# Moving the token choice of a sparse attention layer into the loop of the gated delta rule before it

## The chip, the cores and the metric

The kernel runs on one core of one Trainium2 chip, in one launch, on fp32 data. The time is device time in microseconds (us) of that core. A core has five engines, and each works through its own list of instructions in order: TensorE (PE: matrix products and transposes, with PEld for its weight loads), VectorE (DVE), ScalarE (ACT: functions such as exp and sigmoid), GpSimd (POOL, which here also issues the indirect DMAs) and SyncE (SP, which only issues DMAs). Data meet only through semaphores, so an instruction that is not ready holds back all that stand behind it on its engine.

## The reference

The program is four layers, each added to the residual stream `x` of 8 sequences x 512 tokens x 256 channels after a layer norm: a gated mixer with its MLP, a mixture of eight experts with two per token, a gated delta rule, and an attention over chosen tokens. The last two matter here, cut to what they compute (`B` is 8, `T` 512, `D` 256):

```python
# gated delta rule: 8 heads, keys of 128, values of 64
x_ = layernorm(x)
beta = 2 * sigmoid(x_ @ Wb)
alpha = exp(-exp(A_log) * softplus(x_ @ Wa + dt_bias))
q, k = l2norm(silu(conv4(x_ @ Wq))), l2norm(silu(conv4(x_ @ Wk)))
v = silu(conv4(x_ @ Wv))
for t in range(T):          # state: 64 x 128 per head
    state = alpha[t] * (state - beta[t] * outer(state @ k[t], k[t])) + beta[t] * outer(v[t], k[t])
    out[t] = state @ q[t]
x = x + (out * rsqrt(mean(out * out) + 1e-5) * o_norm_w * silu(x_ @ Wg)) @ Wo

# attention over chosen tokens: 16 heads of 16
z = layernorm(x)
gate = sigmoid(z @ mWg)                 # one number per token
idx = top_k(gate, 256)                  # half of the tokens of each sequence
c = z[idx]
o = softmax((c @ mWq) @ (c @ mWk).T / 4) @ (c @ mWv) @ mWo      # per head
y = zeros(T, D); y[idx] = o * gate[idx]
out = x + y
```

What the attention needs in order to choose its tokens (layer norm, gates, ranks) depends on the delta rule's output of that one sequence, and on nothing of the other sequences.

## The kernel before

The four layers follow one another in one program. Python functions lay down the instructions, and the framework's scheduler fixes each engine's final order, derives the semaphores, and maps tile pools to memory; a pool keeps `bufs` buffers per tag, and a new tile of a tag waits until the oldest one's readers are done. Line numbers are those of the profile of this kernel.

**The delta rule** (`delta_rule`, from L566) takes each sequence in two groups of 4 heads, so it has 16 groups, n = 0 to 15; even n is a sequence's first group, odd n its second. Tokens are cut into 4 tiles of 128. Per group: `channels` ("c" in the order below) projects and convolves (PE `pc` L681, ACT L683, three DVE taps per chunk L685); `norms` ("n") takes the lengths of the keys and queries, through tiles of the tag "sq"; `fade` ("e") makes the decay masks on POOL and PE (L728 and after); `prepare` ("p") makes the 128 x 128 lower triangles of key products, one DVE product per head and tile (`NQ`, L748); `inverses` ("i") inverts the triangles block by block: POOL and ACT copy the diagonal 32-blocks (`own`, L776), DVE turns them (`low`), solves blocks of 8 and 16 rows in a long chain of small operations, and turns the result (`dn`, L763), after which PE multiplies ever larger blocks (`pn` L831 first). `sides` ("v") transposes values and keys (`ptv`, `ptk`, then the DVE products `r` and `K`, L914); `advance` ("a") runs the recurrence over the 4 tiles (`pkq` L950, `pw` L957, `state`); `silus` ("g") makes the output gates; `outputs` ("o") squares (`oq`, a tile of a tag with one buffer), normalises (L988 to L996), projects and adds to the residual tile `cx` (L1009), and after the second group stores the sequence to HBM (`xbufs[1]`, L1012). `load` ("t" or "l") brings in a coming sequence: the residual tile, eight indirect gathers `yg` of the experts' results on POOL with their DVE adds, the layer norm `cz` and its transposes.

While group n advances, group n+1 is prepared and inverted and group n+2 projected. All of these are generators. A string of letters, written by hand, says in which order they are stepped within one group of the loop; what is left is drained at the group's end. The string sets the order in which instructions are laid down, from which the scheduler makes each engine's list.

**The attention** (`chosen_attention`, from L1100) is a pipeline over the sequences with six parts, each a generator, at lags of 0 to 5 steps: `norm` loads a sequence `dx` and centres it (`dz`), one step ahead of the others; `place` (lag 0) transposes `dz` (`ptd`, L122), multiplies it with the gate weights repeated over 128 columns (`gate_all`, PE `pgt` L1167), so that every partition holds the gates of all 512 tokens as a row, takes the sigmoid, extracts the gates as a column (POOL product with the identity `dg` L1171, DVE reduction), ranks each token by comparing its gate with all the others (`ahead`, and `rank` L1186, once per tile of 128 tokens), and scatters the rows of `dz` to their ranks in HBM (`placed`, four indirect DMAs on POOL, L1193); the first 256 rows are then loaded as `c` (L1195). `project` (lag 1) transposes `c` (`pct` L1207) and makes queries, keys and values; `maxima` (lag 2) takes the row maxima of the scores (`sc` L1250, DVE reductions L1252) and folds them into the queries; `sums` (lag 3) makes the transposed scores, exponentials (ACT) and weighted sums; `finish` (lag 4) divides, projects (`pdy` L1311), stores the result, and gathers each token's row of it (`got`, L1317 on POOL; a token that was not chosen gets a row of zeros); `leave` (lag 5) multiplies by the gate, adds to `dx` (L1324) and stores the output. A second string of letters orders the parts within a step. The loads and stores of `dx`, `c`, `result` and the output are on SP's queue, weights on ACT's.

Of the kernel before, what the change touches and what calls it, by code (L numbers as in the profile page):

```python
# [14 lines left out]
F32 = mybir.dt.float32  # L15
# [5 lines left out]
P = 128  # L21
# [24 lines left out]
def block(ctx: ExitStack, tc: tile.TileContext, a: dict, out: bass.AP):  # L46
# [518 lines left out]

    def delta_rule():  # L566
        with ExitStack() as cx:
# [21 lines left out]
            V.tensor_scalar(wo, wo, onw, None, ALU.mult)  # L589

# [422 lines left out]

            seqs = {}
# [35 lines left out]
            def drain(*work):  # L1050
# [9 lines left out]
                p v t p v p l a v p t l a v p a p a p l a p a p a i l a i g a i c l g i a a e i l a g i e c i a a i l e g e  # L1060
# [13 lines left out]
            for n in range(total):  # L1074
# [4 lines left out]
                if n % 2 == 0 and coming is not None:  # L1079
                    work["t"] = coming  # L1080
                elif n + 3 < total:
                    work["l"] = coming = load(n // 2 + 2)
                else:
                    coming = None
                for k in order:
# [9 lines left out]
                drain(*work.values())  # L1095

# [3 lines left out]
    def chosen_attention():  # L1100
# [4 lines left out]
        with ExitStack() as cx:  # L1105
            wp = cx.enter_context(tc.tile_pool(name="d_w", bufs=1))
            gate_w = wp.tile([P, DK, 1], F32, name="gate_w")
# [4 lines left out]
            for t, n in ((gate_w, "mWg"), (wq, "mWq"), (wk, "mWk"), (wv, "mWv"), (wo, "mWo")):  # L1112
                nc.scalar.dma_start(t, a[n].rearrange("(c p) f -> p c f", p=P))
            gate_all = wp.tile([P, DK, P], F32, name="gate_all")
            V.tensor_copy(gate_all, gate_w.to_broadcast([P, DK, P]))
# [16 lines left out]
            placed = [dram.tile([T, D], F32, name=f"placed{b}") for b in range(B)]  # L1132
# [16 lines left out]
            zs, rows, chosen, qkv, outs, gots = {}, {}, {}, {}, {}, {}  # L1149

            def norm(b):
                x = tk.tile([P, NT, D], F32, name=f"dx{b}", tag="x", bufs=8)
                nc.sync.dma_start(x, rows_of(xbufs[1][b]))
                z = tk.tile([P, NT, D], F32, name=f"dz{b}", tag="z", bufs=3)
                center(sm, x, z, f"d{b}")
                zs[b] = x, z
                yield

            def place(b):


                x, z = zs.pop(b)
                xT = tk.tile([P, DK, T], F32, name=f"dxT{b}", tag="xT")
                turn(pf, "pf", z, xT, f"d{b}")
                ps = pf.tile([P, T], F32, name=f"pgt{b}", tag="pf")
                for k in range(DK):
                    TE.matmul(ps, gate_all[:, k, :], xT[:, k, :], start=k == 0, stop=k == DK - 1)  # L1167
                row = tk.tile([P, NT, P], F32, name=f"row{b}", tag="row")
                S.activation(row, ps, AF.Sigmoid)
# [222 lines left out]
```

## Time and profile before

| what | value |
|---|---|
| median of 3 runs | 3389.84 us (3385.32 to 3393.04) |
| the profiled execution's own time | 3389.93 us |
| its span, from first to last instruction | 3388.2 us |
| mean granted TensorE clock | 0.912 |
| mixer, MLP and experts, 0 to 1520 us | PE busy 1419.7 us |
| delta rule, 1520 to 2918.4 us | PE busy 1224.5, DVE 919.3, ACT 869.2, POOL 316.6 us |
| attention, 2918.4 to 3388.2 us | PE busy 366.6, DVE 208.6, ACT 139.2, POOL 85.4 us |

The profile is of one execution; it lies 1.7 us in span below its own time, and its own time is at the median. An answer by stretches gives, for each, the length, then busy us and the number of instructions of PE, PEld, DVE, ACT and POOL, then the granted TensorE clock (1.00 is full), the busy share of the DMA engines, and GB/s. In a row of waits, the engine and line that wait stand first, then what ended the wait, then us in total, times, and the longest. In a timeline, a row has the start in us, the duration, the engine, the line, the operation with output and inputs, and in brackets the idle time before it with its releaser. In a row of groups, after the bar, stand busy us, mean ns of one, and idle time before. Busy DVE or POOL does not mean that these bound the kernel; what counts is which wait ends last in a stretch.

### The profile page before, as it was taken

The numbers are of one execution on the slowest core, as the hardware profiler recorded it, in microseconds if no ns is written. First come the engines' busy times: TensorE is split into PE (matmuls) and PEld (weight loads), VectorE is DVE, ScalarE is ACT, GpSimd is POOL, SyncE is SP. The second block draws the span as 40 slices with busy tenths as digits, with TensorE's granted clock in tenths as the row PEclk, the third lists the DMA queues.
The fourth block names the chain that finished last, engine by engine and source line by source line (L and its number), as shares of the span: only waits on it lengthen the run. The fifth ranks groups of instructions, "written<-read, shape, count | busy, mean of one in ns | idle before, by whom it ended". The sixth has DMA issues, their size and how long they took to land. (4 is left out here: it accounts for less than half of the span.)

```text
span 3388.2 us, 59510 instructions
## 1 busy us (share of the span) xinstructions
PE 3010.9 (89%) x24662; PEld 2224.0 (66%) x24662; DVE 1891.7 (56%) x4375; ACT 1545.9 (46%) x2747; POOL 632.1 (19%) x669
## 2 busy tenths in 40 slices
PE   7999999889999999995889898989889899498887
PEld 3655555445999999982567666666666667366664
DVE  4555545334555555555557777677776664554432
ACT  3554442112333333335457667667676764233322
POOL 1000003541010000013112313222221110212111
PEclk8999999999999999997779899989899897687787
DMA  5000003220588888881000000000000000201111
GB/s 205 13 25 13 13 13 145 69 70 19 225 324 332 334 328 314 332 322 41 2 1 20 8 20 8 20 8 25 3 23 2 8 2 8 92 24 40 37 40 47
DMA packets 97133, 302.69 MB, mean 89 GB/s; under 512 B 12760, under 2 KB 79456, under 8 KB 87648
## 3 DMA queue, kind: packets, MB, share of 16 engines
q0 software_dynamic: 19440, 221.19, 17.3%
q1 hardware_dynamic: 68016, 68.44, 6.0%
q10 hardware_dynamic: 9408, 9.27, 0.8%
q8 instruction: 194, 3.18, 0.4%
q14 instruction: 75, 0.61, 0.1%
HBM read 248.79 MB, written 50.08 MB: 88 GB/s over the span
## 5 line engine op out<-in xcount | busy, mean ns | idle before, releaser
L444 PE MATMUL p_r<-zT,w 128*128 128x128 f32 x4544 | 534.4, 276 | 7.1 <-DMA w<-in_experts,wrow 6.7
L444 PEld LDWEIGHTS p_r<-zT,w 128*128 128x128 f32 x4544 | 526.4, 192 | 12.5 <-issue 7.8
L685 DVE SCALAR_TENSOR_TENSOR cy<-pc,conv,cy 128x509 f32<-128x509 f32 (+2 forms) x480 | 351.4, 740 | 141.5 <-ACT cy L683 136.5
L448 ACT ACTIVATE t_r<-p_r,w 128x128 f32<-128x128 f32 x568 | 170.4, 373 | 266.5 <-PE p_r L444 181.6
L444 PE MATMUL p_s<-sxT,shared_w 128*128 128x512 f32 x512 | 222.8, 595 | 1.7 <-ACT sxT L124 1.7
L449 DVE SCALAR_TENSOR_TENSOR l_r<-p_r,w,t_r 128x128 f32<-128x128 f32 x284 | 79.9, 343 | 175.6 <-PE p_r L444 175.6
L444 PEld LDWEIGHTS p_s<-sxT,shared_w 128*128 128x128 f32 x512 | 96.9, 191 | 121.7 <-issue 108.1
L508 POOL DMA_INDIRECT w<-in_experts,wrow x71 | 67.0, 943 | 579.6 <-ACT sg_r L457 568.3
L681 PE MATMUL pc<-cxT,wq 128*128 128x512 f32 x256 | 153.1, 724 | 15.8 <-DVE cy L685 13.6
L681 PE MATMUL pc<-cxT,wk 128*128 128x512 f32 x256 | 143.5, 654 | 7.2 <-DVE cy L685 3.9
L304 PE MATMUL pp<-hT,win 128*128 128x512 f32 x320 | 144.3, 603 | 0.2 <-ACT hT L126 0.2
L522 PE MATMUL pyr<-w,htr 128*128 128x256 f32 x568 | 134.5, 380 | 2.6 <-DVE htr L462 2.6
L449 DVE SCALAR_TENSOR_TENSOR g_r<-p_r,w,t_r 128x128 f32<-128x128 f32 x284 | 80.0, 344 | 101.2 <-PE p_r L444 101.2
L683 ACT ACTIVATE cy<-pc,conv 128x512 f32<-128x512 f32 x160 | 108.3, 685 | 60.3 <-PE pc L681 58.9
L728 POOL TENSOR_TENSOR e<-le,g 128x512 f32<-128x512 f32 x64 | 66.5, 1046 | 363.6 <-DVE NQ L748 341.0
L746 PE MATMUL pk<-kq 128*128 128x256 f32 x512 | 130.4, 391 | 0.7 <-DVE NQ L748 0.4
L748 DVE SCALAR_TENSOR_TENSOR NQ<-pk,nbk,e 128x256 f32<-128x256 f32 x256 | 110.0, 477 | 27.4 <-PE pk L746 27.0
L394 PE MATMUL pf<-hT,fc 128*128 128x512 f32 x256 | 122.8, 607 | 0.0
L457 ACT ACTIVATE sg_r<-g_r 128x512 f32<-128x512 f32 x71 | 44.8, 631 | 159.8 <-DVE g_r L455 159.8
L399 PE MATMUL pj<-pj,sT 128*128 128x256 f32 x512 | 113.1, 379 | 0.0
L522 PEld LDWEIGHTS pyr<-w,htr 128*128 128x128 f32 x568 | 102.5, 190 | 13.7 <-issue 2.7
L950 PEld LDWEIGHTS pkq<-state,kq 128*128 128x128 f32 x768 | 95.6, 197 | 24.1 <-DVE state L972 16.7
(393 smaller groups left out, 6217.5 us busy)
## 6 DMA issues: line engine op xcount, KB each, us to landing
zt<-zbuf SPq DMA_DIRECT2D x71, 128.0 KB
ybuf<-yt SPq DMA_DIRECT2D x71, 128.0 KB, 3.2
zbuf<-zeros SPq DMA_DIRECT2D x11, 768.0 KB, 11.0
x<-in_x SPq DMA_DIRECT2D x8, 512.0 KB
xbuf<-x SPq DMA_DIRECT2D x8, 512.0 KB, 2.9
sx<-xbuf SPq DMA_DIRECT2D x8, 512.0 KB, 3.9
xbuf<-sx SPq DMA_DIRECT2D x8, 512.0 KB, 2.9
cx<-xbuf SPq DMA_DIRECT2D x8, 512.0 KB, 9.4
```

Of the source, the lines that this page charges most:

```text
L304: TE.matmul(ps, win[:, k, m : m + P], hT[:, k, :], start=k == 0, stop=k == DK - 1)
L394: TE.matmul(ps, fc[:, k, f * P : (f + 1) * P], hT2[:, k, :], start=k == 0, stop=k == DK - 1)
L399: TE.matmul(ps, sT[:, f, t * P : (t + 1) * P], pj[:, f, :], start=f == 0, stop=f == 7)
L444: last_of[0] = TE.matmul(ps[:, f, :], wx[:, k, (f0 + f) * P : (f0 + f + 1) * P], xin[:, k, :], start=k == 0, stop=k == DK - 1)
L448: S.activation(t3[:, f, :], p3[:, f, :], AF.Identity, bias=b3[:, f0 + f : f0 + f + 1])
L449: V.scalar_tensor_tensor(t1[:, f, :], p1[:, f, :], b1[:, f0 + f : f0 + f + 1], t3[:, f, :], ALU.add, ALU.mult)
L522: last_of[0] = TE.matmul(ps, hT[:, f, :], w2[:, f, :], start=f == 0, stop=f == 3)
L681: TE.matmul(ps, w[:, k, n * P : (n + 1) * P], xT[:, k, :], start=k == 0, stop=k == DK - 1)
L683: S.activation(y, ps, AF.Copy, scale=conv[:, at + n, 3:4])
L685: V.scalar_tensor_tensor(y[:, j:], ps[:, : T - j], conv[:, at + n, 3 - j : 4 - j], y[:, j:], ALU.mult, ALU.add)
L746: TE.matmul(pk[:, j, :, :], kq[:, h + j, 0, ts], kq[:, h + j, :, ts], start=True, stop=True)
L748: V.scalar_tensor_tensor(NQ[:, :, t * HG + h + j, :], pk[:, j, :, :], s.nbk[:, t, h + j : h + j + 1], bc(e[:, h + j, :], 1, 2), ALU.mult, ...
```

## The change

The token choice of a sequence leaves the attention and is done in the delta rule's loop. The new `place` gets the residual tile `cx` of a sequence whose second group is done, still in memory, and works for it during the next sequence's first group: for n = 2, 4, ..., 14 it places sequence n/2 - 1. The last sequence is placed after the loop. Its steps are the letter "w", which is put into the order at seven places, all of them early (only even groups have such work).

How the gates are made changes too: instead of a transposition and PE products, DVE multiplies `dz` by the gate weights, loaded repeated over the partitions, and sums over the channels, which gives the gates as a column; ACT takes the sigmoid in place; PE turns the column, repeated to 128 columns, into the row by four transposes, and ACT copies it. Ranking and scattering are as before. The tiles share buffers with the delta rule's: `dz` the tag of `oq` and `cz`, the products and the row the tag "sq", `ahead` that of the inverses' "tmp", the transposes the banks of `ptv`, `ptk` and the others.

Gates and clipped ranks are kept for all sequences in tiles that last (`seat_gate`, `seat`), and `placed` is allocated ahead of both layers. In the attention, `norm` and `place` are replaced by `fetch`, which issues the loads of `c` and `dx` one step ahead; `gate_all` and its matmuls go, the lags shrink by one, and the loop has B + 4 steps. `dx` has 7 buffers, not 8.

```diff
+    seat_gate = [cst([P, NT], f"sgate{b}") for b in range(B)]
+    seat = [const.tile([P, NT], mybir.dt.int32, name=f"seat{b}") for b in range(B)]
+    placed = [dram.tile([T, D], F32, name=f"placed{b}") for b in range(B)]
...
+            gate_w = wp.tile([P, D], F32, name="gate_w")
+            nc.scalar.dma_start(gate_w, a["mWg"].rearrange("d o -> (d o)").partition_broadcast(P))
...
+            def place(b, x):
+                z = tk.tile([P, NT, D], F32, name=f"dz{b}", tag="oq")
+                center(sm, x, z, f"d{b}")
+                yield
+                prod = ch.tile([P, NT, D], F32, name=f"dg{b}", tag="sq", bufs=2)
+                V.tensor_mul(prod, z, bc(gate_w, 1, NT))
+                col = seat_gate[b]
+                V.tensor_reduce(col, prod, AX.X, ALU.add)
+                S.activation(col, col, AF.Sigmoid)
+                pt = pt_.tile([P, NT, P], F32, name=f"prow{b}", tag="pt")
+                for t in range(NT):
+                    TE.transpose(pt[:, t, :], col[:, t : t + 1].to_broadcast([P, P]), ident)
+                row = ch.tile([P, NT, P], F32, name=f"row{b}", tag="sq", bufs=2)
+                S.copy(row, pt)
+                yield
+                rank = sm.tile([P, NT], F32, name=f"rank{b}", tag="rank")
+                for t in range(NT):
...
+                    V.tensor_reduce(rank[:, t : t + 1], ahead.rearrange("p t s -> p (t s)"), AX.X, ALU.add)
+                    yield
...
+                V.tensor_copy(seat[b], rank)
+                for t in range(NT):
+                    G.indirect_dma_start(placed[b], bass.IndirectOffsetOnAxis(ap=at[:, t : t + 1], axis=0), z[:, t, :], None)
+                yield
...
-                p v t p v p l a v p t l a v p a p a p l a p a p a i l a i g a i c l g i a a e i l a g i e c i a a i l e g e
+                p w v t w p v w p w l a v w p t l a w v p w a p a p l a p a p a i l a i g a i c l g i a a e i l a g i e c i a a i l e g e
...
+                if n % 2 == 0 and n > 0:
+                    work["w"] = place(n // 2 - 1, done)
...
+                done = s.x
+            drain(place(B - 1, done))
...
-            gate_all = wp.tile([P, DK, P], F32, name="gate_all")
-            V.tensor_copy(gate_all, gate_w.to_broadcast([P, DK, P]))
...
+            def fetch(b):
+                c = chosen[b] = tk.tile([P, NS, D], F32, name=f"c{b}", tag="c")
+                nc.sync.dma_start(c, placed[b][0:C1, :].rearrange("(s p) d -> p s d", p=P))
+                x = tk.tile([P, NT, D], F32, name=f"dx{b}", tag="x", bufs=7)
                 nc.sync.dma_start(x, rows_of(xbufs[1][b]))
...
+                rows[b] = x, seat_gate[b], seat[b]
...
-            parts = {"p": (place, 0), "s": (sums, 3), "m": (maxima, 2), "q": (project, 1), "f": (finish, 4), "l": (leave, 5)}
...
-            for n in range(B + 5):
+            parts = {"s": (sums, 2), "m": (maxima, 1), "q": (project, 0), "f": (finish, 3), "l": (leave, 4)}
+            fetch(0)
+            for n in range(B + 4):
+                if n + 1 < B:
+                    fetch(n + 1)
...
-                for k in "p s q l m f p s q f m f s f p s q m q p s q m p m s q p m n f".split():
+                for k in "s q l m f s q m f m s f s q m q s q m m s q m f".split():
```

The old `norm` and `place` of the attention, and the `z`, `xT`, `dg` and `ahead` tiles that they used there, are taken out; the work of `project`, `maxima`, `sums`, `finish` and `leave` stays as it was.

## The prediction

> **What bounds the kernel now.** I read the page's busy shares first, then the stages by time, then the waits of the two stages that the change touches, then their timelines.
>
> ```profile
> PE 3010.9 (89%) x24662; PEld 2224.0 (66%) x24662; DVE 1891.7 (56%) x4375; ACT 1545.9 (46%) x2747; POOL 632.1 (19%) x669
> ...
> 2323.00:2368.00 45.00, 44.90 (x281) 35.33 (x280) 34.01 (x89) 27.31 (x39) 18.34 (x19) 1.00 0.13 42
> 2368.00:2376.50 8.50, 0.31 (x10) 0.17 (x13) 8.43 (x16) 5.51 (x8) 6.30 (x5) 0.69 0.10 31
> 2376.50:2390.00 13.50, 11.65 (x398) 8.52 (x400) 7.97 (x18) 10.77 (x17) 0.00 (x0) 0.56 0.02 4
> ...
> PE pn L831 <- DVE dn L763: 47.1, 7, 8.4
> ...
> 2357.35 2.17 POOL L776 COPY own<-NQ 32x512 f32<-32x512 f32 x2 [1.34 <-DVE NQ L748]
> ...
> 2375.64 0.70 DVE L763 STREAM_TRANSPOSE dn<-cols 128x512 f32<-128x512 f32 x1
> ...
> 2917.96 0.42 DVE L1009 TENSOR_TENSOR cx<-py,cx 128x256 f32<-128x256 f32 x1 [1.44 <-PE py L1008]
> ...
> 2952.87 0.98 POOL L1193 DMA_INDIRECT placed<-dz,at  x1 [1.71 <-DMA placed<-dz,at]
> ...
> 2955.54 0.96 POOL L1193 DMA_INDIRECT placed<-dz,at  x1 [1.70 <-DMA placed<-dz,at]
> ...
> 2963.50 1.09 PE L1207 MATMUL pct<-ident,c 128*128 128x128 f32 x4 [20.40 <-DMA c<-placed]
> ...
> 2925.00:2960.00 35.00, 8.26 (x24) 4.16 (x24) 30.48 (x117) 10.23 (x16) 8.10 (x8) 0.60 0.48 152
> ...
> L1186 DVE TENSOR_REDUCE rank<-ahead 128x1 f32<-128x512 f32 x32 | 21.7, 677 | 0.2
> ...
> L1167 PE MATMUL pgt<-dxT,gate_all 128*128 128x512 f32 x32 | 17.2, 657 | 1.0 <-ACT dxT L124 1.0
> ...
> L122 PE MATMUL ptd<-ident,dz 128*128 128x128 f32 x64 | 10.2, 298 | 15.9 <-DVE dz L115 15.6 <-ACT row L1169 0.2
> ```
>
> PE is the busiest engine, but the stages differ. The delta rule runs from about 1524 to 2918 us in 161 us per sequence (the stores of a finished sequence start at 2162.6, 2323.5, 2484.1). The three stretches are the start of one sequence's first group, the place that receives the new work. For 45 us PE is full (44.9) at clock 1.00, while DVE is busy 34.0: DVE has 11.0 us free. Then PE stands still for 8.2 us. The wait names the cause: the first small matmul of the blockwise inverse (L831) waits for the DVE transpose `dn`, and DVE is full (8.43 of 8.50). The chain is: last NQ product on DVE, its diagonal copied by POOL and ACT (`own`, 2357.35), a long DVE chain, `dn` at 2375.64. All first groups but one show the gap: 8.2, 8.4, 8.2, 8.2, 8.2, 4.6 and 1.4 us from the second sequence to the eighth; their sum is the 47.1 us of the wait. So in this very stretch DVE, not PE, sets the end.
>
> The chosen attention runs from the last add at 2918.4 to 3388.2. The first 45.1 us of it, to the first `pct` transpose at 2963.50, are the normalising, ranking and scattering of the first sequences with PE at 8.26 us of 35. After that PE works 83 to 88% of each 50 us.
>
> [...] after the 8.2 us gap the clock is 0.56 for 13.5 us. [...] the page's loads show 1283 ns. [...] a scatter of 0.97 us is followed by the next only 2.67 us after its start, since it waits for the landing.
>
> **The change part by part.** *Out of the attention's startup.* The last sequence's placing is not overlapped: it is drained after the loop, and in the built order the load of `c0` waits for that sequence's fourth scatter to land, though its own data are long there, because its buffer lies where the closed pools were; all of SP's later loads and PE's `pct` are behind it. So the startup shrinks and does not vanish. From 2918.4: last statistics 0.57, root 0.30, reciprocal 0.17, four `dz` 1.36, product 1.22, reduction 1.21 (the 1024-wide one at L992), table load and sigmoid 1.50, four transposes 0.8, row copy 0.59, ranking 6.2 (7.6 by the rows below, less the overlap of neighbours), cast 0.18, four scatters one landing after another 10.7 (4 x 2.67), load 2.8. Sum 27.6, against 45.1: gain 17.5.
>
> *Out of the attention's steps.* PE loses the turning (10.2) and the gate matmuls (17.2), 27.4 in all, of which 8.26 are in the startup: 19.1 remain. Two table loads a sequence (9.0 + 6.4 us on ACT) go, which hold back the exponentials that free the score banks; I take 1 us for each of six sequences, 6. DVE's ranking goes too, but DVE was mostly off the path. A stall stays: each full step stops PE at the second half's scores (7.3, 5.6, 4.4, 6.1, 2.0, 4.4 us), because DVE holds the add of the gathered result ahead of the maxima. In the new order this add stands at the head of the next step, again about 10 us after its output; I take no change, bounds +15 and -15. Fewer pipeline stages: the step that goes is the startup, already counted. Gain 42.5, bounds 28 to 58. The `dx` and `c` loads move on SP's queue; their 5 us land far ahead of use.
>
> *Into the delta rule, seven times.* DVE per sequence, by the attention's rows over 8: statistics and `dz` (12.2 + 4.7 + 1.3 + 11.9)/8 = 3.8; product 1.2; reduction 1.2; ranking (21.7 + 11.6 + 10.9, and 16.7 for the comparisons of 128 to 384 columns)/8 = 7.6; casts 0.5. Together 14.3, and 12.3 of occupancy, as 34 neighbours overlap by some 0.06 (four `dz` take 1.36, not 1.62). PE gets four transposes, 0.45; ACT 2.4 with one more table load, under PE's work. The scatters' bytes fall where DMA is 5% busy.
>
> DVE is in order, and the built order puts all of it between the previous sequence's last add and NQ's second half. There 11.0 us are free, but in pieces that wait for PE. I walk the new order with these durations, in us from that add (2322.97), in brackets where the trace of before has the same instruction end:
> - `dz` done 6.9, product 8.5, reduction 10.0, sigmoid after its table load 12.7.
> - PE reaches the four transposes at 14.4. They wait for the sigmoid; `ptv`, `ptk` and `pab` are queued behind them. Row copied 15.6; ranks done 19.5, 22.4, 25.8, 28.7, each with the step's own DVE work between.
> - `r` 22.8 (17.6), so `pw` waits 2.0 on PE; `state` 29.2 (22.2), `pkq` waits 1.0; `g` 30.8 (26.9); last NQ 37.8 (34.3), 3.6 late.
> - POOL: scatters at 29.6, 33.4 (two fade products between), 36.1, 38.8, each waiting for the landing before it. Behind them stand the third fade product, `own` and the gathers. `own` ends 42.3 (36.6), 5.7 late; DVE's `low` waits for it.
> - From `low` to `dn` the built order also has the output's reduction and a convolution tap (1.2 + 0.7), which stood behind `dn` before: 7.6 late. The next sequence's gathers start at 46.9 and land 3 later; their adds stand in the inverse's chain, where DVE comes at 47.0 and, with a part made good later, loses 2.1: 9.7, say 9.5.
>
> What is late next is `pn`, PE's next work, and with it the rest of the sequence, in which PE is nearly full: nothing there gives it back. Five sequences at 9.5 are 47.5; the seventh place has no gathers of a next sequence beside it, the eighth no convolutions either: 7.5 and 5. Loss 60. From below: all 11.0 free us are used, the excess is 1.3, with the 1.9 moved ahead 3 each, 21. From above: nothing is hidden, 12.3 + 1.9 = 14 each, 98.
>
> The gate weights' broadcast load lies among a dozen loads on ACT's queue at the stage's start: 0.5.
>
> Sum: 3389.9 (the profiled execution, span 3388.2 and 1.7 around it; the median is 3389.8) + 60 - 42.5 = 3407.
>
> **The rivals.** *DVE swallows it, faster:* the ranking fills DVE's holes and the loss is about 3 each, 21, with a gain of 47: 3364. For it: DVE is 72% busy over the sequence (115.6 of 161). Against: only the 45 us before the gap count. It decides from a loss under 6 us per sequence (42.5 over 7). *POOL becomes the bound, slower:* the scatters, each behind the landing of the one before, hold `own`, the fades and the gathers, 14 each, 98, gain 42: 3446. For it: 10.7 us of POOL per sequence where a group has few holes. Against: before, POOL is busy 18 of these 45 us. *The two cancel:* about 6 each, 3390; DVE's holes take half.
>
> **How the numbers follow.** Forecast 3407, own range 3397 to 3432, chance 0.45; POOL bound 0.15; swallowed 0.27; cancel 0.13. Under 0.2% (7 us) a measurement of this kernel can't tell a change. Faster 0.27, same 0.13, slower 0.60. For 8 in 10 I leave out the outer parts of the first two rivals: 3361 to 3441.
>
> **What would show it.** The gap before `pn` in first groups grows from 8 to 11 or more, and the distance of stores from 161 to about 170; `own` starts just after the fourth scatter; the first `pct` comes 28 us after the last add, not 45; from there to the end about 400 us instead of 425. I am wrong if the gap stays near 8 (then faster), if `c0` doesn't wait for the scatters, or if the stall at the scores goes or doubles.

## The result, and the profile after

The changed kernel takes 3419.22 us (median of 4 runs, 3411.78 to 3426.13), the kernel before 3391.23 (median of 4). The ratio is 1.0083, 95% interval 1.0068 to 1.0099: slower by 0.8%. The profiled execution is the fastest of the four, 3411.78 us with a span of 3409.8, so its sums stand 7.4 us below the median.

By stages, in the two profiled executions:

| stage | before | after | difference |
|---|---|---|---|
| to the last add of the delta rule | 2918.4 | 3000.0 | +81.6 |
| from there to the first `pct` | 45.1 | 29.8 | -15.3 |
| from there to the end | 424.7 | 380.0 | -44.7 |
| span | 3388.2 | 3409.8 | +21.6 |

The page of the changed kernel, then busy time by stretches: three of the first group of the fifth sequence (the one shown of before; it now begins at 2361.6), and the attention from its first `pct`.

```profile
PE 3011.3 (88%) x24598; PEld 2206.6 (65%) x24598; DVE 1907.1 (56%) x4382; ACT 1531.9 (45%) x2732; POOL 630.2 (18%) x661
...
2361.60:2401.20 39.60, 37.86 (x238) 30.16 (x235) 33.49 (x90) 21.57 (x35) 9.80 (x11) 1.00 0.11 37
2401.20:2413.00 11.80, 8.68 (x43) 5.30 (x42) 7.26 (x19) 7.96 (x11) 9.41 (x10) 1.00 0.11 33
2413.00:2425.10 12.10, 0.09 (x5) 0.04 (x6) 12.10 (x21) 4.48 (x7) 7.52 (x7) 0.60 0.15 43
3029.80:3409.80 380.00, 331.57 (x2272) 222.61 (x2272) 124.10 (x208) 107.79 (x201) 40.09 (x48) 0.84 0.15 44
```

Before, PE was full for 45 us and then stood still for 8.2. Now it has 46.5 us of work in 51.4 and then stands still for 12.1, with DVE at 12.10 of 12.10. The waits give the sum over all groups, 66.1 us in place of 47.1, with the same seven waits; the timeline shows the cause in this group.

```profile
PE pn L840 <- DVE dn L772: 66.1, 7, 13.0
...
2361.14 0.42 DVE L1018 TENSOR_TENSOR cx<-py,cx 128x256 f32<-128x256 f32 x1
...
2390.79 1.06 POOL L1058 DMA_INDIRECT placed<-dz,at  x1 [0.16 <-DVE rank L1055]
...
2397.63 0.96 POOL L1058 DMA_INDIRECT placed<-dz,at  x1 [1.71 <-DMA placed<-dz,at]
...
2400.30 1.01 POOL L1058 DMA_INDIRECT placed<-dz,at  x1 [0.64 <-DMA placed<-dz,at]
2401.32 1.07 POOL L785 COPY own<-NQ 32x512 f32<-32x512 f32 x1
2402.86 1.05 POOL L785 COPY own<-NQ 32x512 f32<-32x512 f32 x1 [0.48 <-DMA placed<-dz,at]
...
2406.49 1.13 PE L739 MATMUL pe<-e,gt 128*128 128x512 f32 x2 [2.23 <-POOL e L737]
...
2411.57 0.48 DVE L1078 SCALAR_TENSOR_TENSOR cx<-yg,wts,cx 128x256 f32<-128x256 f32 x1 [1.66 <-DMA yg<-ybuf,rows]
...
2424.31 0.70 DVE L772 STREAM_TRANSPOSE dn<-cols 128x512 f32<-128x512 f32 x1
2425.06 1.90 PE L840 MATMUL pn<-dn,NQ 32*32 32x16 f32 x128 [12.01 <-DVE dn L772]
```

From the end of the last add (2361.6) to the start of `dn` it was 52.2 us and is 62.7, 10.5 more. The two halves of `own` (L785) stand behind the fourth scatter: the first starts at 2401.32, as that scatter ends (2401.31), while the last NQ product ended at 2398.72; POOL's fade product, behind the scatters too, keeps PE waiting for 2.23 us; in the inverse's chain on DVE, from `low` to `dn`, now lie six adds of the next sequence's gathers in place of four, one of which waits 1.66 us for its landing, and the output's sum `oms` with a convolution's tap, which stood behind `dn`.

The attention's start, from the timeline:

```profile
2999.62 0.42 DVE L1018 TENSOR_TENSOR cx<-py,cx 128x256 f32<-128x256 f32 x1 [0.77 <-PE py L1017]
...
3023.92 0.97 POOL L1058 DMA_INDIRECT placed<-dz,at  x1 [1.70 <-DMA placed<-dz,at]
...
3026.73 0.36 SPq L1200 DMA_DIRECT2D c<-placed  x1
...
3029.75 1.09 PE L1212 MATMUL pct<-ident,c 128*128 128x128 f32 x4 [22.66 <-DMA c<-placed]
```

The load of `c` is issued when the last sequence's fourth scatter has landed, 27 us after the last add, although the first sequence's rows have been in HBM since long before.

### The profile page after: what moved, and what is told of

It reads as the page before. It is cut to its first block, busy times and chain, and to the rows that moved or that the text cites. A ratio compares the mean times of both kernels' runs of the same rounds, so it can differ in the third digit from the quotient of the medians.

```text
span 3409.8 us, 59488 instructions
## 1 busy us (share of the span) xinstructions
PE 3011.3 (88%) x24598; PEld 2206.6 (65%) x24598; DVE 1907.1 (56%) x4382; ACT 1531.9 (45%) x2732; POOL 630.2 (18%) x661
## 4 chain that ended last, share of the span: by engine, by line
PE 33%; DVE 11%; DMA 4%; issue 3%; ACT 2%; POOL 2%; POOLq 0%; ACTq 0%; DVEq 0%; SPq 0%
PE pc L690 7%; PE pk L755 3%; PE py L1017 2%; PE pkq L959 2%; PE st L1276 2%; DMA placed<-dz,at 2%; DVE cy L694 2%; PE pqk_True L1225 1%; PE sc L1255 1%; PE pw L966 1%; PE pn L885 1%; PE pu L894 1%; PE pn L710 1%; PE pow L985 1%; DMA yg<-ybuf,rows 1%
## 5 line engine op out<-in xcount | busy, mean ns | idle before, releaser
L444 PEld LDWEIGHTS p_r<-zT,w 128*128 128x128 f32 x4544 | 525.3, 192 | 11.3 <-issue 5.8
L690 PE MATMUL pc<-cxT,wq 128*128 128x512 f32 x256 | 146.2, 696 | 11.6 <-DVE cy L694 9.4
L1257 DVE TENSOR_REDUCE maxs<-sc 128x2 f32<-128x512 f32 x128 | 79.9, 684 | 100.9 <-PE sc L1255 100.9
L692 ACT ACTIVATE cy<-pc,conv 128x512 f32<-128x512 f32 x160 | 108.2, 686 | 60.1 <-PE pc L690 58.5
L757 DVE SCALAR_TENSOR_TENSOR NQ<-pk,nbk,e 128x256 f32<-128x256 f32 x256 | 111.0, 477 | 29.8 <-PE pk L755 29.3
L522 PEld LDWEIGHTS pyr<-w,htr 128*128 128x128 f32 x568 | 103.1, 192 | 14.4 <-issue 2.7
```

Of the source, the lines that this page charges most:

```text
L444: last_of[0] = TE.matmul(ps[:, f, :], wx[:, k, (f0 + f) * P : (f0 + f + 1) * P], xin[:, k, :], start=k == 0, stop=k == DK - 1)
L522: last_of[0] = TE.matmul(ps, hT[:, f, :], w2[:, f, :], start=f == 0, stop=f == 3)
L690: TE.matmul(ps, w[:, k, n * P : (n + 1) * P], xT[:, k, :], start=k == 0, stop=k == DK - 1)
L692: S.activation(y, ps, AF.Copy, scale=conv[:, at + n, 3:4])
L757: V.scalar_tensor_tensor(NQ[:, :, t * HG + h + j, :], pk[:, j, :, :], s.nbk[:, t, h + j : h + j + 1], bc(e[:, h + j, :], 1, 2), ALU.mult, ...
```

## The experiments

How a stage's length repeats has to be known first. In one and the same loop the second groups take 72 us or 76: PE idles for about 4 us in either, but is granted less clock around their small products in the longer ones. These are the same 18 us of the second group of the fifth sequence, first in the changed kernel, then in `last_apart`, whose loop is the same.

```profile
2490.00:2508.00 18.00, 14.42 (x305) 9.60 (x304) 16.76 (x32) 13.96 (x20) 4.76 (x4) 0.91 0.01 2
```

```profile
2490.00:2508.00 18.00, 14.54 (x263) 10.64 (x264) 13.51 (x23) 11.37 (x15) 4.74 (x4) 0.73 0.01 2
```

The clock was 0.91 in one and 0.73 in the other. In `last_apart` twelve executions lie between 3382 and 3408 us. So ends of the delta rule that differ by less than some 20 us aren't read here. The distance from a group's last add to `dn` is read: in each of the five full sequences (n = 2 to 10) it repeats to 0.2 us between these two runs (62.6 to 63.8 us in `last_apart`, 62.7 to 63.7 in the changed kernel).

All runs, with the places in their profiled executions in us. "Startup" is the time from the delta rule's last add to the first `pct`, "rest" the time from there to the end. Each ratio is to executions of the kernel before that were taken beside the run; their medians lie between 3384.9 and 3391.2 us, so a comparison of two runs by their medians can be off by a few us.

| run | median | ratio to before | delta rule ends | add to `dn` | startup | rest |
|---|---|---|---|---|---|---|
| before | 3388 | 1 | 2918.4 | 52.2 | 45.1 | 424.7 |
| changed | 3419.2 | 1.0083 | 3000.0 | 62.7 to 63.7 | 29.8 | 380.0 |
| no_place | 3324.8 | 0.983 | 2915.4 | 52.2 to 52.7 | 13.0 | 392.6 |
| no_rank_scatter | 3331.7 | 0.9842 | 2924.2 | 57.0 to 57.7 | 11.9 | 394.5 |
| no_rank | 3374.6 | 0.9954 | 2962.6 | 57.9 to 60.1 | 19.6 | 395.5 |
| no_scatter | 3369.1 | 0.9953 | 2956.3 | 59.7 to 61.3 | 19.1 | 382.4 |
| scatter_free | 3402.7 | 1.004 | 2996.9 | 60.3 to 61.4 | 25.5 | 383.5 |
| last_apart | 3388.6 | 1.001 | 3007.8 | 62.6 to 63.8 | 12.5 | 386.0 |
| gates_dve | 3365.9 | 0.9936 | 2917.8 | as before | 45.4 | 400.7 |
| before_adds_pool | 3368.1 | 0.9955 | 2912.9 | as before | 45.1 | 405.8 |
| act_ranks_pool | 3355.9 | 0.9901 | 2987.5 | 58.8 to 62.5 | 11.5 | 380.0 |
| hybrid12 | 3345.7 | 0.9878 | 2916.9 | as before | 22.0 | 405.2 |
| hybrid12_f | 3356.3 | 0.9916 | 2920.7 | as before | 22.7 | 410.3 |
| stay_f | 3368.9 | 0.9947 | 2918.6 | as before | 46.1 | 402.4 |

### What of the placing costs the delta rule its 82 us

**no_place.** The edit, beside the constants that stand for gates and places:

```diff
-                    work["w"] = place(n // 2 - 1, done)
+                    nc.sync.dma_start(rows_of(placed[n // 2 - 1]), done)
...
-            drain(place(B - 1, done))
+            nc.sync.dma_start(rows_of(placed[B - 1]), done)
```

> The changed kernel with nothing of the placing in the loop or behind it: no norm, gates, ranks or scatters for any sequence; the residual rows go to `placed` in their order by one SP store, gates are 0.5 and places fixed. So the attention works on the first 256 rows of the residual. If the placing itself is the whole loss in the delta rule, that stage ends where it did before, at 2918 us (not 3000), and the gap ahead of the inverse's first product is back at 8.2 us. The attention then starts about 6 us after the last add (a store landing and a load) and takes 380 us from there: 3306 us in all. If instead the shared buffers, the order or the changed memory layout cost time, the stage ends after 2930.

The delta rule ended at 2915.4, `dn` is back at 52.2 to 52.7, the gap at 8.1 to 8.6. So the whole loss is the placing's; layout and the order's empty slots cost nothing. The startup was 13.0, not 6, and the rest 12.6 longer than 380. The three runs with fixed places are all at 392 to 396, those of the changed attention with true ranks at 380 to 386; the last gathers read other rows there, and why this takes longer is open.

**no_scatter.**

```diff
-                for t in range(NT):
-                    G.indirect_dma_start(placed[b], bass.IndirectOffsetOnAxis(ap=at[:, t : t + 1], axis=0), z[:, t, :], None)
+                nc.sync.dma_start(rows_of(placed[b]), z)
```

> The changed kernel with the four scatters per sequence replaced by one SP store of the rows in their order (the attention works on the wrong 256 rows); norm, gates and ranks are still made. The forecast's walk: `own` is then held only by the last NQ product, 3.6 instead of 5.7 us late, while the gathers of the next sequence stay behind `own` in the built order; per sequence 7.4 of 9.5 us remain, so the delta rule ends near 2918 + 0.78 x 82 = 2982. The POOL rival: more than half of the 82 us goes, the stage ends before 2960. DVE alone: no change, 3000. The startup of the attention is shorter by three landings, 8 us, in any case.

**no_rank.** The comparisons and sums are taken out, and `rank` is set from a constant.

```diff
-                    V.tensor_reduce(rank[:, t : t + 1], ahead.rearrange("p t s -> p (t s)"), AX.X, ALU.add)
+                V.tensor_scalar(rank, order_at, 1.0, None, ALU.mult)
```

> The changed kernel without the comparisons and sums of the ranks (7.6 us of DVE per sequence); places are fixed, in the order of the rows, so that the four scatters stay, on the wrong places. The forecast's walk: DVE is left with some 5 us of placing, which its 11 us of holes take in, and the scatters come early enough not to hold `own`: 3 us per sequence remain, the delta rule ends near 2940. The POOL rival: 10.7 us of POOL per sequence are still there, so more than half of the loss stays, the stage ends after 2960. The startup of the attention is shorter by 6 us.

**no_rank_scatter** has both edits.

> The changed kernel with neither ranks nor scatters: only the norm, the gates and the row are made in the loop, and the rows go to `placed` in their order by one SP store (the attention works on the wrong 256 rows). With no_scatter (+38 us in the delta rule) and no_rank (+44) it closes a square with the changed kernel (+82). If ranks and scatters are the whole cost, the stage ends at 2918 to 2922 us. If what is left, some 7 us of DVE work and a longer hold of the residual tile `cx` (the next sequence's load is issued 6.2 us after the last add and not 2.8, so that its gathers and adds come later), costs time by itself, each first group is still 3 to 5 us longer and the stage ends near 2945; the two parts then overlap in the changed kernel.

The four corners by the end of the delta rule: +5.8 with neither, +37.9 with ranks alone, +44.2 with scatters alone, +81.6 with both. An estimate from the medians, less each profile's startup and rest and the 1.7 to 2.0 us around the span, gives +8, +49, +41 and +88. By it the changed kernel and last_apart, whose loop is the same, lie 17 us apart, so it is no finer than the ends. Either way the runs with one of the two are some 30 to 40 us longer than the run with neither, more than these ends repeat to, and norm and gates alone cost 6 or 8. DVE alone as the cause falls, since ranks without scatters cost 44 us less than both; the forecast's 78% and 3 us per sequence fall too. The POOL rival's two marks were met, but by 4 and 3 us, less than the ends repeat to; what speaks against POOL alone is that ranks without scatters still cost 38.

That the parts nearly add up does not make them clean parts. In no_rank the scatters run 4.6 to 14.4 us after the last add (29.2 to 38.7 in the changed kernel, fifth sequence), and `own` ends only 0.5 us late. Its `dn` is late because the chain from `low` to `dn` takes 21.2 to 22.4 us (16.0 before), with four convolution taps in it. So its 44 us are not what the forecast has scatters cost, `own` held behind their landings; they belong to another built order.

By `dn` the parts look otherwise: 4.7 to 5.4 us later with neither, 7.5 to 8.9 with ranks alone, 5.7 to 7.9 with scatters alone, 10.5 to 11.3 with both. The walk's 7.4 for no_scatter was right to 0.2 in four of five sequences. So lateness at `dn` alone does not give the loss: in no_rank_scatter `dn` is 5 us late and the stage loses 6 in all.

PE's own time shows what it leaves out. This is PE alone, from the first group's last add to the end of the delta rule, in the kernel before and in the changed one: length, PE's busy time and products, clock, DMA share, GB/s.

```profile
1765.30:2918.40 1153.10, 1040.14 (x12736) 0.91 0.04 11
```

```profile
1765.50:3000.00 1234.50, 1072.77 (x12764) 0.89 0.04 14
```

| run, over this stretch | PE idle, us | PE busy, us |
|---|---|---|
| before | 113.0 | 1040.1 |
| no_place | 108.7 | 1041.3 |
| no_rank_scatter (neither) | 117.3 | 1039.2 |
| no_scatter (ranks alone) | 141.0 | 1049.9 |
| no_rank (scatters alone) | 131.9 | 1062.0 |
| scatter_free | 147.7 | 1080.5 |
| changed | 161.7 | 1072.8 |
| last_apart (same loop) | 155.1 | 1092.6 |

The placing makes PE idle 48.8 us longer and busy 32.6 us longer, of which the 28 added transposes are 4.4. So a third of the loss is not waiting: the same products take longer, at clock 0.89 in place of 0.91. The idle time repeats to 7 us between the two runs with the same loop, the busy time only to 20. With ranks alone 28.0 of 37.8 us are idle time, with scatters alone 18.9 of 40.8. These are single executions: that the scatters lower the clock is not shown by them.

In no_rank the wait is also at another place. Its timeline, PE and DVE:

```profile
2404.12 3.75 PE L692 MATMUL pc<-cxT,wq 128*128 128x512 f32 x4 [10.98 <-DVE cy L696]
...
2406.89 0.69 DVE L774 STREAM_TRANSPOSE dn<-cols 128x512 f32<-128x512 f32 x1
```

The built order has a convolution's product ahead of `pn`, and it is this that waits 10.98 us, for a tap which stands in DVE's list beside the inverse's chain. In the five full sequences no gap above 1.5 us is left at `pn`, and nothing is gained by it: a wait is booked on whatever PE has next.

**scatter_free.**

```diff
-                    G.indirect_dma_start(placed[b], bass.IndirectOffsetOnAxis(ap=at[:, t : t + 1], axis=0), z[:, t, :], None)
+                    G.indirect_dma_start(placed[b][t], bass.IndirectOffsetOnAxis(ap=at[:, t : t + 1], axis=0), z[:, t, :], None)
```

> The changed kernel with each of a sequence's four scatters going to a buffer of its own, so that none waits for the landing of the one before; the attention loads the first 256 rows of the residual in place of the scattered ones, so its choice of tokens is not made. Ranks and scatters stay in the loop. The scatters cost 38 us of the delta rule's 82 (no_scatter). If the 1.7 us of landing ahead of three of four scatters, with POOL's later work queued behind them, are this cost, the stage ends between 2960 and 2972. If POOL's issue time, or the scatters as such beside DVE, is the cost, it stays above 2985.

POOL in its timeline, the group that starts at 2364.6:

```profile
2395.15 0.98 POOL L1058 DMA_INDIRECT placed<-dz,at  x1 [0.30 <-issue]
2396.43 0.97 POOL L1058 DMA_INDIRECT placed<-dz,at  x1 [0.30 <-issue]
...
2402.37 2.17 POOL L785 COPY own<-NQ 32x512 f32<-32x512 f32 x2
```

The scatters follow one another in 1.3 us, not 2.7, `low` starts 40.3 us after the last add, as in no_scatter, and `dn` is at 60.3: at this place the landings' waits are 2.4 of the 3.0 us of the scatters. Yet the stage ended at 2996.9, inside the expectation of the other theory (above 2985), and its second groups took 76 us. The median fell by 16.6 us, or by 12.6 when each is set against the kernel before beside it; the startup gave 4.3 of it, the rest took 3.5 more. So by the medians the landings' waits cost the delta rule some 12 to 16 us, and PE's idle time agrees with 14.0. Most of the scatters' share is not their waits. Against no_scatter, 6.8 us of PE's idle time remain and 30.5 of busy time, for the same 12,764 products at clock 0.88 in place of 0.91. Part of this is chance, since the profile of no_scatter is the fastest of its executions and that of scatter_free one of the slowest; why the products take longer beside scatters stays open.

### What the attention gained

**last_apart.** The last sequence is placed by the same function in the attention's second step, from a tile loaded again.

```diff
-            drain(place(B - 1, done))
...
+            last = tk.tile([P, NT, D], F32, name="last", tag="last", bufs=1)
+            nc.sync.dma_start(last, rows_of(xbufs[1][B - 1]))
...
+                if n == 1:
+                    at_work["p"] = place(B - 1, last, gate_w, sm, tk, tk, pf, tk, "pf")
```

> The changed kernel, its whole computation, but the last sequence is placed inside the attention's second step, from a row tile that is loaded again and with buffers of the attention, instead of behind the loop. If the wait of the first load of `c` for that placing is what fills the startup of 29.7 us, it falls to about 7 us, and the step that takes the placing up gets 3 to 5 us longer: 3419 - 22 + 4, about 3400 us. If something else bounds the startup (weight loads that wait for the closed pools, the last store), the startup stays above 15 and the time above 3408.

```profile
3007.34 0.42 DVE L1056 TENSOR_TENSOR cx<-py,cx 128x256 f32<-128x256 f32 x1 [1.44 <-PE py L1055]
...
3015.44 0.36 SPq L1201 DMA_DIRECT2D c<-placed  x1
...
3020.32 1.09 PE L1213 MATMUL pct<-ident,c 128*128 128x128 f32 x4 [13.02 <-DMA result<-zero]
```

The startup is 12.5 us, not 29.8, and the rest 6.0 longer. So the wait for the scatters filled 17 us. That it is not a wait for the data shows in scatter_free: there `c` is loaded from the residual, which needs no scatter, and its first load still waits for the scatters, with the first `pct` 25.5 us after the last add; what is left is the buffer. The median of last_apart is 3388.6, a ratio of 1.001 (0.9995 to 1.0025): the time of the kernel before. It is 25 to 31 us below the changed kernel's, as one compares ratios or medians, and the attention accounts for 11.3 of these; the others are in the delta rule, whose loop is the same, and are not explained.

**gates_dve.** In the kernel before, in the attention:

```diff
-                turn(pf, "pf", z, xT, f"d{b}")
-                ps = pf.tile([P, T], F32, name=f"pgt{b}", tag="pf")
-                for k in range(DK):
-                    TE.matmul(ps, gate_all[:, k, :], xT[:, k, :], start=k == 0, stop=k == DK - 1)
+                V.tensor_mul(prod, z, bc(gate_w, 1, NT))
+                V.tensor_reduce(col, prod, AX.X, ALU.add)
```

> The kernel before with one part of the change alone: the gates are made by the DVE product and sum and four PE transposes, in the attention, in place of the transposition of `dz` and the PE products; ranking and scattering stay in the attention. PE loses 27.4 us of work and gets 8 x 0.45. If PE's work sets the pace of the attention's steps, as the forecast's 19.1 us say, the attention takes 450 to 456 us, not 470, and the time is about 3372. If the stalls at the scores set it, less than 6 us are gained, above 3383.

The time is 3365.9, and the rest 24.0 us shorter, a little more than expected. So over half of the 44.7 us that the change gains there come from the gates alone, with ranking and scatters still in the attention. The other 20.7 came when these left it too and the pipeline lost a stage; no run separates these.

**before_adds_pool.**

```diff
-                    V.scalar_tensor_tensor(x[:, t, :], got[:, t, :], col[:, t : t + 1], x[:, t, :], ALU.mult, ALU.add)
+                    G.tensor_scalar(got[:, t, :], got[:, t, :], col[:, t : t + 1], None, ALU.mult)
+                    G.tensor_add(x[:, t, :], got[:, t, :], x[:, t, :])
```

> The kernel before with the last adds of the attention (gathered result times gate, plus residual) as a product and a sum on POOL, not on DVE, where they held the maxima. If the 30 us of PE's stalls at the second half of the scores (7.3, 5.6, 4.4, 6.1, 2.0, 4.4) are due to these adds, they go and the attention gets 25 to 35 us shorter[...]: 3355 to 3365. If DVE is late for other reasons, or POOL now holds back the scatters and gathers, the time stays above 3380.

None of the six stalls at the scores is left, and PE's idle time from the first `pct` falls from 66.3 to 46.3 us. The median fell by 19.1, less than the 25 expected. By stretches, from the first `pct` to the end, of before, gates_dve and before_adds_pool in this order:

```profile
2963.50:3388.20 424.70, 358.38 (x2344) 251.12 (x2344) 173.03 (x360) 128.63 (x229) 72.10 (x79) 0.79 0.13 38
```

```profile
2963.20:3363.80 400.60, 345.19 (x2296) 243.12 (x2296) 186.18 (x393) 123.14 (x225) 64.27 (x74) 0.80 0.13 40
```

```profile
2958.00:3363.80 405.80, 359.47 (x2344) 247.93 (x2344) 159.15 (x329) 128.64 (x229) 124.53 (x143) 0.80 0.13 40
```

gates_dve takes 13.2 us from PE's busy time and 10.9 from its idle time; before_adds_pool takes 20.0 from the idle time and nothing from the busy time. The changed kernel, shown above, has 331.57 us busy in 380.0: 26.8 busy and 17.9 idle less than before, at clock 0.84 in place of 0.79. Its stalls are not the same ones: no wait for the maxima is left at the scores (`sc`), where six of 2.0 to 7.3 us stood. Five of 2.3 to 3.1 us stand at the transposed scores (`st`), two of them for the last adds (`dx`). PE's first one of before, then the first two of the changed kernel, from the timelines:

```profile
3086.27 3.86 PE L1250 MATMUL sc<-dk,dq 32*128 32x256 f32 x16 [7.28 <-DVE maxs L1252]
```

```profile
3144.64 2.07 PE L1276 MATMUL st<-dq,dk 32*128 32x256 f32 x4 [3.11 <-DVE maxs L1257]
...
3188.59 2.07 PE L1276 MATMUL st<-dq,dk 32*128 32x256 f32 x4 [2.26 <-DVE dx L1329]
```

### Versions put together from this

**act_ranks_pool.** In place of the comparisons:

```diff
+        for t in range(NT):
+            S.activation(prod[:, 0:2, :].rearrange("p a d -> p (a d)"), row.rearrange("p t s -> p (t s)"), AF.Sign, bias=col[:, t : t + 1], scale=-1.0, accum_out=rank[:, t : t + 1])
+        V.tensor_scalar(rank, rank, -0.5, (T - 1) / 2, ALU.mult, ALU.add)
```

> The whole computation, put together from what the first runs showed. The last sequence is placed inside the attention's second step (as in last_apart); the ranks are made by ACT from the gates' arguments (the sign of the difference to every other, summed along the row, four instructions a sequence), so that DVE loses the comparisons and sums; the sigmoid stands behind, off the chain; the scatters' step comes later in the order of letters; the attention's last adds are on POOL. DVE has 6.5 us of placing per sequence instead of 14.3, and in the built order seven of eight adds of the next sequence stand ahead of the inverse's chain. Forecast: 3 to 5 us per sequence in the delta rule, which ends near 2945; attention 399 less 10 by the adds: 3335. If ACT[...] or POOL becomes the bound, the stage ends after 2965 and the time is above 3360.

The time is 3355.9, 1.0% faster than before and 63 us faster than the changed kernel, between the two expectations, but the delta rule isn't where the forecast had it. The profiled execution is the slowest of four (3381.2), so that its end, 2987.5, says little; `dn` at 58.8 to 62.5 says that most of the lateness is still there. Its chain from `low` to `dn` is short (17.1 us against 20.3), but six gathers' adds now stand ahead of the last NQ product, which comes at 39.7 to 42.0 in place of 37.1. Taking the ranks off DVE moved the bound within the group. Of the 63 us, 18 are in the attention (startup and rest 391.5 against 409.8); the other 45 are, by the medians, in the delta rule. Some 20 of these last_apart has too, without the ranks on ACT; which step gave the others is not shown.

**hybrid12.**

```diff
+                if n == 12:
+                    work["w"] = place(5, done)
...
+            seqn = [5] + [b for b in range(B) if b != 5]
```

> The whole computation, from the kernel before: only one sequence, the sixth, is placed in the delta rule's loop (at n = 12, where the changed kernel's first group grew by 3.9 us alone), and the attention begins with it; the other seven are placed in the attention, where DVE is busy 41% of the time, with the gates by DVE (as in gates_dve) and the last adds on POOL (as in before_adds_pool). If the loop's cost is by the sequence, and the attention hides the placing once PE no longer turns and multiplies for it, the delta rule ends near 2922, the first transposes of `c` follow 12 us later, and the rest takes about 382: 3318 us. If the placing of the second sequence, which the first step now has beside the first sequence's projections, holds the next step up, the startup's 33 us come back in part: 3330 to 3350.

The time is 3345.7, 1.2% faster than before, the fastest version that computes everything. The group n = 12 grew by 4.7 us, the next one is 2.6 shorter, and the delta rule ends where it did (2916.9). The startup is 22.0, not 12, the rival's case: the first `pct` stands in PE's list behind the second sequence's gates. But the larger part of the miss is the rest, 405.2 us where 382 were expected: the two changes of the attention gave together no more than one of them alone (400.7 and 405.8). Why is not shown.

```profile
2937.93 1.12 PE L1216 MATMUL prow<-ident,col 128*128 128x128 f32 x4 [21.52 <-ACT col L1213]
...
2938.84 1.06 PE L1252 MATMUL pct<-ident,c 128*128 128x128 f32 x4
```

**hybrid12_f** and **stay_f** change the letters of the attention; stay_f has no place in the loop at all.

```diff
-                for k in "p s q l m f p s q f m f s f p s q m q p s q m p m s q p m n f".split():
+                for k in "p s q l m f p s q m f m s f s p q m q s p q m m p s q m p n f".split():
```

> hybrid12, the whole computation, with the attention's letters in the changed kernel's relative order of maxima and finishing (one finishing step fewer before the maxima). In the changed kernel the last three projected outputs lie 46.8, 26.5 and 8.1 us apart, in hybrid12, as in the kernel before, 41.0, 35.0 and 22.7. If that comes from the order of letters, the tail gets some 17 us shorter: 3329 us. If it comes from the pipeline's lags or from the placing that is gone, no change, 3346.

> The whole computation with nothing moved into the delta rule: the kernel before with the gates by DVE, the last adds on POOL and the order of letters of hybrid12_f, all in the attention. The delta rule ends at 2918 us, the startup of 45 us stays. If the changes of the attention add up (24 by the gates, 19 by the adds, up to 17 by the order), the time is 3388 - 43 = 3345, or 3328 with the order. If they share the same stalls, 3352 to 3360. Against hybrid12_f it tells what moving one sequence is worth: 23 us of startup less 3 to 5 in the loop, or nothing if the first step takes it back.

With these letters the last three outputs of hybrid12_f lie 43.7, 24.3 and 9.6 us apart, so the tail does come from the letters; but the first output comes 134.0 us after the first `pct`, where it came after 115.0. What the tail gains the start loses, and the time is 10.7 worse: of the 9.7 us between the two profiled executions 5.8 are in the attention, the others in the delta rule, whose instructions are the same. Against stay_f, one sequence placed in the loop is worth 12.5 us. gates_dve and before_adds_pool do not seem to add up: they gain 21 and 19 us alone, and stay_f, with both and the new letters, gains 16. If the letters cost it the same 10.7, the two gain an estimated 27 together.

## Why the prediction was right, and where it was not

The forecast was 3407; the measured median 3419.22 lies in its own range, and the change is slower, as foreseen. The profiled execution is 4.8 us above the sum. Below that lie two errors of about 20 us that nearly cancel: the delta rule lost 81.6 us and not 60, the attention gained 60.0 and not 42.5. The mechanism was largely right; that the sum came so close was luck.

*The walk to `dn`, right.* Last NQ product 3.6 us late by the forecast, 3.2 measured; `own` 5.7, measured 6.2; from `low` to `dn` 4.0, measured 4.3; in all 9.5, measured 10.5 to 11.3 in the five full sequences. The mechanism is the one foreseen at each step: scatters behind their landings, `own` behind them, the next sequence's adds in the chain. The gap itself grew to 10.4 to 13.0, and the stores of finished sequences, 161 us apart before, came to lie 170 to 177 us apart, as the text had it; where PE waits earlier is not `pw` and `pkq` but a fade product (2.23 us).

*The step from lateness to loss, right for the waiting, with a term left out.* PE alone over the seven first groups, before and then changed: the sum of their lengths, PE's busy time in them, and its mean.

```profile
sum 579.90, PE 513.20; mean PE 73.31
```

```profile
sum 666.80, PE 544.59; mean PE 77.80
```

PE's idle time in them grew by 55.5 us, where the forecast had 60; in the five full sequences by 46.1, where it had 47.5. This is the loss that the walk reckons, and "nothing there gives it back" is nearly so: the second groups idle 6.8 us less. What the sum has at nothing is that the products themselves take longer: the busy time of the first groups grew by 31.4 us, 4.4 of them the added transposes. The prediction had read the low clock behind the gap (0.56) and gave it no term. That lateness at `dn` sets the loss does not hold as a rule: no_rank_scatter loses 6 us in all with `dn` 5 late in each of five.

*The last places, mis-sized.* 7.5 and 5 us were taken beside the seventh and eighth sequence (n = 12 and 14); 5.2 and 18.7 were measured. The term that failed is "no convolutions either: 5". Of the 18.7 us, PE's idle time is 7.2: the last NQ product comes 7.2 us late, not 3.2, `dn` 12.9, and two waits of `pw` are 6.8 us where one of 2.1 stood. The other 11.5 are busy time: 7.4 in this group, at clock 0.68 in place of 0.75, and 4.1 in the last group, which has no placing at all (0.69 in place of 0.75). In the last group these 4 us stand in every run that scatters in all seven places, and in no other; why is open.

*The startup, right.* 27.6 by the sum, 29.8 measured; the wait of `c` for the fourth scatter is there, and last_apart shows 17 us of it to be due to it. In the changed kernel's startup the product of 1024 columns, 1.22 in the sum, which no trace of before shows, takes 1.23 (L1030; the 512-wide `K` of before takes 0.69), the table load ahead of the sigmoid 1.28 (L1033), and the scatters start 2.67 to 2.74 us apart, the second to the fourth after a wait of 1.70 or 1.71 for the landing of the one before.

*The attention's steps, mis-sized.* 25 us by the forecast, 44.7 measured; the total gain, 60.0, is beyond the upper bound of 58. The term that failed is "I take no change" for the stalls at the scores. They went, one of the forecast's own signs of being wrong, and shorter ones came elsewhere: waits of PE above 1.5 us fell from 32.2 to 17.7 us after the first outputs. Besides, 26.8 us of busy time went, where the removed instructions are 18.8, at clock 0.84 in place of 0.79. gates_dve shows that taking PE's gate work out shortens the idle time too, by 10.9; it doesn't show the second part, since its busy time fell by 13.2, less than the 15.2 of the products that it saves. In the delta rule of before the clock was 0.56 for the 13.5 us behind an idle time of 8.2, and one might look to PE's stalls for the slow products here. But before_adds_pool took all six stalls away and left the busy time as it was (359.47 against 358.38 us, clock 0.80 against 0.79). So what raised the clock in the changed attention stays open.

*The rivals.* "DVE swallows it" falls: with everything but scatters the loss is still 38 us. "POOL becomes the bound" at 14 us per sequence is not shown as a whole: about half of the loss goes with the scatters, not all, and of that half only some 12 to 16 us are the waits for their landings. "The two cancel" falls with the ratio.

## What to carry to other kernels

Free time of an engine, averaged over a loop, is no room for new work: look for the stretch in which the new work lands, ask which in-order queue it stands in front of, and who waits behind it. Reckon busy time as well as waits: here a third of the loss was the same products taking longer. Ask next whether the old place could be made cheap: here the placing disturbed the attention through 27 us of PE work and through one add that held the maxima, and after changing those two in place, and moving only one sequence of eight to shorten the pipeline's start, the kernel is 1.2% faster, where moving all eight made it 0.8% slower. And a load into a buffer that lies where earlier tiles lay can wait for those tiles' last readers, though its own data are long there: here the first load of `c` was issued 27 us after the last add, and the wait filled 17 us of the startup.

## What was not expected of the hardware

Executions of one program differ by up to 26 us (last_apart, 3382 to 3408); in two profiled executions with the same loop the granted clock around the small 32 x 32 products was 0.73 and 0.91 over the same 18 us. The ranks and the scatters, each added alone to the run with neither, made `dn` only some 2 us later per sequence, and the stage 32 and 38 us longer. ACT made a token tile's ranks over 512 columns in 0.71 us plus 0.19 for reading the sum out, and no table load stands between the sigmoid at 2372.04 and the first of them, as act_ranks_pool's timeline shows:

```profile
2372.04 0.20 ACT L589 ACTIVATE sgate<-logit 128x4 f32<-128x4 f32 x1
2372.15 0.57 ACT L586 COPY row<-prow 128x512 f32<-128x512 f32 x1
2374.11 0.20 ACT L683 ACTIVATE beta<-pab 128x32 f32<-128x32 f32 x1 [1.39 <-PE pab L681]
2374.20 0.71 ACT L591 ACTIVATE dg<-row,logit 128x512 f32<-128x512 f32 x1
2374.81 0.19 ACT L591 ACTIVATION_READ_ACCUMULATOR dg<-row,logit 128x1 f32 x1
```
